# A convolution over normalized images: the next image's first points carried in the group matmul, bias by pairs, and one row of the last store in fourteen pieces

## The chip, the cores and the metric

The kernel runs on one core of a Trainium2 chip. The metric is the device time of one execution in microseconds; the median of 14 runs stands for the kernel. A separate, profiled execution gives the views that are read below; its span is counted from the first instruction to the last.

## The reference

The input x has 8 images of 32 channels and 128 x 128 points, in float32. Each image is group-normalized (16 groups of two channels, mean and variance over the group), convolved with a 3 x 3 kernel, a bias is added, and x itself is added:

```python
def _gn(v, G=16, eps=1e-5):
    g = v.reshape(B_, G, C_ // G, H_, W_)
    m = jnp.mean(g, axis=(2, 3, 4), keepdims=True)
    s = jnp.var(g, axis=(2, 3, 4), keepdims=True)
    return ((g - m) / jnp.sqrt(s + eps)).reshape(v.shape)

x = x + _L0_conv_ref(_gn(x), L0_conv_weight, L0_conv_bias, 1, 1)
```

The convolution of the reference is done by Fourier transform with a padding to 256 and a crop that is shifted against an ordinary "same" convolution. Of the cropped result only a corner holds products of the image; elsewhere the convolution is zero and the output is x plus the bias.

## The kernel before

**Layout.** The host arranges x so that a partition is one channel and one of the four parities of row and column: 32 x 4 = 128 partitions, each with H x W = 64 x 64 points of an image. Two images lie side by side as a pair, so there are NPAIR = 4 pairs and B = 8 images. Only the upper left N x N = 33 x 33 points of each image receive a convolution; the lower 31 rows ("low") and the right 31 columns of the upper 33 rows ("right") receive the bias alone.

**Loads and stores.** SyncE (SP) issues all of both, in one queue. Image 0 and image 1 come in halves of 1 MB, images 2 and 3 whole (2 MB), pairs 2 and 3 whole (4 MB each). All of x stays in the core's memory and is updated in place. Pairs 0 and 1 are stored whole, images 4, 5 and 6 one by one, image 7 in two parts: its low rows (`to[:, N:H, :]`), then the upper 33 rows (`to[:, 0:N, :]`), which is the last transfer.

**Statistics.** For each image VectorE sums the points (L275) and ScalarE the squares of the points less an origin (L294). The origin is the group's mean of the first point of each partition, the "pilot": GpSimd (POOL) copies the first points to a small tile (`take_first`, L247), TensorE multiplies them by the averaging matrix `avg` (`pilot`, L253), and ScalarE brings the product back (`pilot_back`, L283). Then `group` (L307) multiplies the two sums by `avg`, and a short chain between ScalarE and VectorE (L318 to L335) makes scale and shift. `normalize` (L349) writes the normalized corner g. GpSimd builds `avg` at the start (L205 to L225) and then the matrix of the weights (L440 to L448).

**Products.** `multiply` (L383) makes three chunks of 11 rows, each by four matrix products, into the four products' common place in PSUM; `add` (L399) adds the result and the bias to x on VectorE. `add_bias` (L367) adds the bias to low and right on GpSimd.

**Order.** `Queues` writes each engine's program in the order of the calls and turns dependencies into semaphore waits. In the loop over images TensorE does chunk 0 and three quarters of chunk 1 of image i, then the pilot of image i+2 and the group of image i+1, then the rest of image i. TensorE's instructions of the loop are kept and emitted as a hardware loop over the pairs (`emit_loop`): one common list of waits, whose values rise by a fixed step per pair. Before the loop TensorE runs three filler products of 512 columns (`keep_warm`, L417), set between the pilot of image 0, the two parts of image 0's group and the pilot of image 1:

```python
take_first(0); pilot(0); pilot_back(0); sum_up(0); sum_squares(0)
keep_warm(H // 2, 1, origin_ok[0])
group(0, 0)
keep_warm(H // 2, 1)
...
group(0, 1)
warm_ok = keep_warm(0, 1, w_ok)
pilot(1)
```

(The first five calls are on lines of their own in the kernel.)

Of the kernel before, what the change touches and what calls it, by code (L numbers as in the profile page):

```python
# [30 lines left out]
AF = mybir.ActivationFunctionType  # L31
ALU = mybir.AluOpType

P = 128
EPS = 1e-5
FFT = 256
FILL = 8
# [110 lines left out]
def conv_preact_kernel(nc: bass.Bass, x: bass.AP, wb: bass.AP, out: bass.AP):  # L148
    NPAIR, _, _, H, W = x.shape
    B = 2 * NPAIR  # L150
    C = P // 4
    LO = (FFT - 2 * H) // 4 - 1
    N = H - LO
# [3 lines left out]
    def sbuf(name, *shape):  # L157
        return nc.alloc_sbuf_tensor(name, list(shape), F32).ap()
# [36 lines left out]
    NUMBERS = 8 * H * W  # L195
    pair = sbuf("pair", P, P // 2, 2)
    w_sb = sbuf("w_sb", P, 4 * P)
    eps = sbuf("eps", P, 1)
    avg = sbuf("avg", P, P)
    warm = sbuf("warm", P, 1)  # L200
    idle = sbuf("idle", P, 1)
    bias_sb = sbuf("bias_sb", P, 1)
    pilots = [sbuf(f"pilot{k}", P, 1) for k in range(2)]
# [12 lines left out]
    sums = put(  # L216
        "pool", lambda e: e.tensor_add(avg[:, 0 : 2 * C], pair2[:, 0 : 2 * C], pair2[:, 2 * C : 4 * C]),
        pair_ok, mark=True,
    )
    sums = put(  # L220
        "pool", lambda e: e.tensor_add(avg[:, 2 * C : 3 * C], avg[:, 0:C], avg[:, C : 2 * C]), sums, mark=True
    )
    for k in (0, 1, 3):
        avg_ok = put(
            "pool", lambda e: e.tensor_copy(avg[:, k * C : (k + 1) * C], avg[:, 2 * C : 3 * C]), sums, mark=True  # L225
        )

    put("act", lambda e: e.activation(warm, eps, AF.Sqrt), eps_ok)  # L228

    gs = [sbuf(f"g{k}", P, N, N) for k in range(2)]  # L230
    sums = [sbuf(f"sums{k}", P, 2, 2) for k in range(2)]
    unused = sbuf("unused", P, H * W)
    origins = [sbuf(f"origin{img}", P, 1) for img in range(B + 1)]
    squares = [sbuf(f"square{img}", P, 1) for img in range(B)]
# [3 lines left out]
    pss = [psum(f"ps{k}", P, NCHUNK, BANK) for k in range(2)]  # L238
    ps_ms = psum("ps_m", P, BANK)
    ps_w = psum("ps_w", P, BANK)  # L240
    first_ok, pilot_ok, origin_ok, sums_ok, group_ok, means_read = {}, {}, {}, {}, {}, {}
    normal, conv_ok, biased, added = {}, {}, {}, {}

    def take_first(img, *needs):

        first_ok[img] = put(
            "pool", lambda e: e.tensor_copy(pilots[img % 2], xts[img][:, 0, 0:1] if img < B else eps),  # L247
            *(rows_in(img, 1) if img < B else ()), *needs, *([pilot_ok[img - 2]] if img > 1 else []), mark=True,
        )

    def pilot(img):
        pilot_ok[img] = put(
            "pe", lambda e: e.matmul(ps_w[:, 0:1], avg, pilots[img % 2], start=True, stop=True),  # L253
            first_ok[img], avg_ok, *([origin_ok[img - 1]] if img else []), mark=True,
        )

    def parts(img):

        return [slice(0, H // 2), slice(H // 2, H)] if img == 0 else [slice(0, H)]
# [8 lines left out]
    def sum_up(img):  # L268
        sums_ok.setdefault(img, [])
        for k, rows in enumerate(parts(img)):  # L270
            piece = xts[img][:, rows, :].rearrange("p h w -> p (h w)")
            sums_ok[img].append(
                put(
                    "dve",
                    lambda e: e.tensor_reduce(sums[img % 2][:, k, 0:1], piece, mybir.AxisListType.X, ALU.add),  # L275
                    *rows_in(img, rows.stop), *([group_ok[img - 2]] if img > 1 else []), mark=True,
                )
            )

    def pilot_back(img):  # L280
        origin_ok[img] = put(
            "act",
            lambda e: e.activation(origins[img], ps_w[:, 0:1], AF.Identity, scale=-float(NUMBERS // 8)),  # L283
            pilot_ok[img], mark=True,
        )

    def sum_squares(img):
        sums_ok.setdefault(img, [])
        for k, rows in enumerate(parts(img)):
            piece = xts[img][:, rows, :].rearrange("p h w -> p (h w)")  # L290
            sums_ok[img].append(
                put(
                    "act",
                    lambda e: e.activation(  # L294
                        unused[:, rows.start * W : rows.stop * W], piece, AF.Square, bias=origins[img],
                        accum_out=sums[img % 2][:, k, 1:2],
                    ),
                    origin_ok[img], *rows_in(img, rows.stop), *([group_ok[img - 2]] if img > 1 else []), mark=True,
                )
            )  # L300

    def group(img, part=0):

        last = len(parts(img)) - 1
        ok = put(
            "pe",
            lambda e: e.matmul(  # L307
                ps_ms[:, 0:2], avg, sums[img % 2][:, part, :], start=(part == 0), stop=(part == last)
            ),
            *(sums_ok[img][part :: last + 1]), avg_ok, *means_read.get(img - 1, ()), mark=part == last,  # L310
        )
        if part == last:
            group_ok[img] = ok
# [43 lines left out]
        pilot_back(img + 1)  # L357
        normal[img].append(origin_ok[img + 1])

    def add_bias(img):  # L360

        xt = xts[img]
        low = xt[:, N:H, :].rearrange("p h w -> p (h w)")
        right = xt[:, 0:N, N:W]
        free = [*normal[img], *sums_ok[img], bias_ok] + ([warm_ok] if img == 0 else [])
        biased[img] = [
            put("pool", lambda e: e.tensor_scalar(part, part, 1.0, bias_sb, op0=ALU.mult, op1=ALU.add), *free, mark=True)  # L367
            for part in (low, right)
        ]

    def multiply(img, n, products=range(4)):
        g = gs[img % 2]
# [33 lines left out]
    def store(to, of, *needs):  # L406
        return put("sp", lambda sp: sp.dma_start(to, of), *needs, adds="stored")
# [5 lines left out]
    def keep_warm(first, times, *needs):  # L413
        piece = xts[0][:, first : first + FILL, :].rearrange("p h w -> p (h w)")
        for _ in range(times):
            ok = put(
                "pe", lambda e: e.matmul(ps_w, avg, piece, start=True, stop=True),  # L417
                *rows_in(0, H), *needs, mark=True,
            )
        return ok  # L420

    take_first(0)
    pilot(0)
    pilot_back(0)
    sum_up(0)
    sum_squares(0)
    keep_warm(H // 2, 1, origin_ok[0])
    group(0, 0)
    keep_warm(H // 2, 1)

# [10 lines left out]
    for q in range(4):  # L441
        rin, cin = q // 2, q % 2
        to = slice(q * C, (q + 1) * C)
        bias_ok = put("pool", lambda e: e.tensor_copy(bias_sb[to, :], wb_sb[:, 15 * C : 15 * C + 1]), weights_in, mark=True)
        for dc, c, b in places[cin]:
# [5 lines left out]
                ),  # L451
                w_zero, weights_in, mark=True,
            )
    take_first(1, w_ok)
    group(0, 1)
    warm_ok = keep_warm(0, 1, w_ok)
    pilot(1)
    take_std(0)
    normalize(0)
    take_first(2)  # L460
    add_bias(0)
    sum_squares(1)
    sum_up(1)

# [3 lines left out]
    for img in range(B):  # L468
        multiply(img, 0)
        multiply(img, 1, range(3))  # L470
        if img:
            add(img - 1, 0, NCHUNK)
            if img == 2 or img == 4:
                store(out[img // 2 - 1], pairs[img // 2 - 1], *finished(img - 2, img - 1))
            elif img > 4:
                store(out[(img - 1) // 2, :, (img - 1) % 2], xts[img - 1], *finished(img - 1))
        pilot(img + 2)
        group(img + 1)
        multiply(img, 1, range(3, 4))
        if img + 1 < B:  # L480
            take_std(img + 1)
            normalize(img + 1)
            take_first(img + 3)
            add_bias(img + 1)
        multiply(img, 2)
        if img + 2 < B:
            sum_squares(img + 2)
            sum_up(img + 2)
        elif img + 2 == B:
            sum_nothing(B)  # L490
    xt, to = xts[B - 1], out[NPAIR - 1, :, 1]
    store(to[:, N:H, :], xt[:, N:H, :], biased[B - 1][0])
    add(B - 1, 0, 2)
    add(B - 1, 2, NCHUNK)
    stored = store(to[:, 0:N, :], xt[:, 0:N, :], biased[B - 1][1], *added[B - 1])


    put.emit_loop(NPAIR, {"act": 2 * 5, "dve": 2 * 5, "pool": 2 * 3})


    seen = {**put.seen["sp"]}
# [43 lines left out]
```

## Time and profile before

| what | value |
|---|---|
| median of 14 runs | 83.79 us (83.56 to 84.25) |
| the profiled execution's own time | 83.72 us |
| its span | 82.4 us |
| busy: TensorE, VectorE, ScalarE, GpSimd | 67.8, 50.1, 48.1, 32.2 us |
| DMA: moved, mean rate | 33.63 MB, 408 GB/s |
| chain that ended last: TensorE, DMA, ScalarE, VectorE | 74%, 8%, 7%, 3% |

Busy time is the time in which an engine had an instruction of its own under way. "PEld" is TensorE's weight load, which overlaps its products. The page divides the span into 40 slices and gives for each the busy share in tenths, and for DMA the mean share of 16 DMA engines. The chain of waits starts at the last compute instruction and follows it back to what released it; it ends where compute ends, and stores behind that are not in it. Windows give the same sums for any stretch of time. "SPq" is SyncE's queue, which only issues transfers.

### The profile page before, as it was taken

To read this page: it belongs to the slowest core of one execution; us is meant where nothing else is said; L and a number is where in the kernel's file an instruction comes from. 1 tells how busy PE (TensorE), PEld (TensorE's weight loads), DVE (VectorE), ACT (ScalarE), POOL (GpSimd) and SP (SyncE) were. 2 spreads that over 40 slices of the span, in tenths; PEclk is the share of its full clock that TensorE was granted. 3 is DMA by queue.
4 is the path that set the end of the run, shared out by engine and by line. 5 is a ranking of instruction groups with operands and counts; after the bars stand their busy time and mean duration, and the time that the engine had idled before them with its cause. 6 is when DMAs were issued, how large, how long until landed. Compare 5 with 4: busy or idle time off the path is not lost.

```text
span 82.4 us, 727 instructions
## 1 busy us (share of the span) xinstructions
PE 67.8 (82%) x238; PEld 43.1 (52%) x238; DVE 50.1 (61%) x43; ACT 48.1 (58%) x55; POOL 32.2 (39%) x52
## 2 busy tenths in 40 slices
PE   0002899898999999999999999999999999999000
PEld 0002455566666666676676666666766766665000
DVE  0019823990799399939967993999399636000700
ACT  6106942997699379739946993797399462000000
POOL 6709700009568000963920680095039106700000
PEclk9999999999999999999999999999999999999975
DMA  2899999999969969989969989989979999999994
GB/s 48 306 401 418 421 425 437 453 429 406 581 286 509 509 286 477 509 350 414 509 270 493 461 366 445 509 366 398 509 334 445 421 422 437 425 437 405 420 402 180
DMA packets 2209, 33.63 MB, mean 408 GB/s; under 512 B 256, under 2 KB 288, under 8 KB 416
## 3 DMA queue, kind: packets, MB, share of 16 engines
q1 hardware_dynamic: 2208, 33.62, 96.8%
q14 instruction: 1, 0.01, 0.0%
HBM read 16.84 MB, written 16.78 MB: 408 GB/s over the span
## 4 chain that ended last, share of the span: by engine, by line
PE 74%; DMA 8%; ACT 7%; DVE 3%; SPq 1%; issue 1%; ACTq 0%
PE ps L383 65%; DMA x<-x_dram 8%; PE ps_w L417 5%; ACT unused L294 5%; PE ps_m L307 3%; ACT g L349 2%; DVE x L399 2%; PE ps_w L253 1%; SPq L175 1%; ACT std L329 0%; ACT square L318 0%; DVE var L323 0%; DVE rstd L335 0%; DVE rstd L332 0%; ACT origin L283 0%
## 5 line engine op out<-in xcount | busy, mean ns | idle before, releaser
L383 PE MATMUL ps<-g,w_sb 128*128 128x363 f32 (+1 forms) x192 | 59.1, 463 | 0.2 <-ACT g L349 0.2
L383 PEld LDWEIGHTS ps<-g,w_sb 128*128 128x128 f32 x192 | 35.2, 189 | 19.4 <-ACT origin L283 1.6
L275 DVE TENSOR_REDUCE sums<-x 128x1 f32<-128x4096 f32 (+1 forms) x9 | 35.4, 3937 | 6.2 <-DMA x<-x_dram 6.2
L367 POOL TENSOR_SCALAR x<-x,bias_sb 128x1984 f32<-128x1984 f32 (+1 forms) x16 | 24.3, 1527 | 18.1 <-ACT origin L283 13.7
L294 ACT ACTIVATE unused<-x,origin 128x4096 f32<-128x4096 f32 (+1 forms) x9 | 30.0, 3330 | 0.3
L399 DVE SCALAR_TENSOR_TENSOR x<-ps,bias_sb,x 128x1089 f32<-128x1089 f32 (+2 forms) x9 | 10.9, 1219 | 7.9 <-PE ps L383 7.9
L349 ACT ACTIVATE g<-x,rstd 128x1089 f32<-128x1089 f32 (+2 forms) x9 | 10.7, 1203 | 3.9 <-DVE rstd L335 3.9
L247 POOL COPY pilot<-x 128x1 f32<-128x1 f32 x8 | 1.5, 184 | 20.3 <-DMA x<-x_dram 20.3
L253 PEld LDWEIGHTS ps_w<-pilot,avg 128*128 128x128 f32 x20 | 4.1, 209 | 9.0 <-POOL pilot L247 6.2
L253 PE MATMUL ps_w<-pilot,avg 128*128 128x1 f32 x20 | 3.1, 224 | 6.2 <-POOL pilot L247 6.2
L323 DVE TENSOR_SCALAR var<-ps_m,square 128x1 f32<-128x1 f32 x8 | 1.8, 219 | 10.5 <-ACT square L318 10.5
L417 PE MATMUL ps_w<-x,avg 128*128 128x512 f32 x6 | 6.0, 1108 | 1.8 <-DMA x<-x_dram 1.8
L318 ACT ACTIVATE square<-ps_m,origin 128x1 f32<-128x1 f32 x8 | 2.1, 261 | 8.7 <-PE ps_m L307 8.7
L307 PEld LDWEIGHTS ps_m<-sums,avg 128*128 128x128 f32 x20 | 3.8, 221 | 2.4 <-issue 1.9
L283 ACT ACTIVATE origin<-ps_w 128x1 f32<-128x1 f32 x9 | 1.4, 152 | 4.6 <-PE ps_w L253 4.6
L307 PE MATMUL ps_m<-sums,avg 128*128 128x2 f32 x20 | 3.8, 258 | 0.3 <-ACT unused L294 0.3
L329 ACT ACTIVATE std<-var,eps 128x1 f32<-128x1 f32 x8 | 2.4, 294 | 2.3 <-DVE var L323 2.3
L332 DVE RECIPROCAL rstd<-std 128x1 f32<-128x1 f32 x8 | 1.3, 164 | 2.9 <-ACT std L329 2.9
L417 PEld LDWEIGHTS ps_w<-x,avg 128*128 128x128 f32 x6 | 1.6, 325 | 1.9 <-issue 1.9
L448 POOL COPY w_sb<-wb_sb 32x128 f32<-32x128 f32 (+1 forms) x8 | 2.5, 339 | 0.0
L335 DVE TENSOR_SCALAR rstd<-ps_m,rstd 128x1 f32<-128x1 f32 x8 | 1.7, 218 | 0.3
L228 ACT ACT_TABLE_LOAD x1 | 1.3, 1283 | 0.8 <-PEq L534 0.8
(17 smaller groups left out, 7.0 us busy)
## 6 DMA issues: line engine op xcount, KB each, us to landing
x<-x_dram SPq DMA_DIRECT2D x2, 4096.0 KB, 33.5
out_dram<-x SPq DMA_DIRECT2D x2, 4096.0 KB, 15.1
out_dram<-x SPq DMA_DIRECT2D x3, 2048.0 KB, 7.3
x<-x_dram SPq DMA_DIRECT2D x4, 1024.0 KB, 7.8
x<-x_dram SPq DMA_DIRECT2D x2, 2048.0 KB, 17.4
out_dram<-x SPq DMA_DIRECT2D x1, 1056.0 KB, 4.5
out_dram<-x SPq DMA_DIRECT2D x1, 992.0 KB, 9.2
wb_sb<-wb_dram SPq DMA_DIRECT2D x1, 62.0 KB, 5.0
```

Of the source, the lines that this page charges most:

```text
L253: "pe", lambda e: e.matmul(ps_w[:, 0:1], avg, pilots[img % 2], start=True, stop=True),
L275: lambda e: e.tensor_reduce(sums[img % 2][:, k, 0:1], piece, mybir.AxisListType.X, ALU.add),
L294: lambda e: e.activation(unused[:, rows.start * W : rows.stop * W], piece, AF.Square, bias=origins[img], accum_out=sums[img % 2][:, k, 1:2],),
L307: lambda e: e.matmul(ps_ms[:, 0:2], avg, sums[img % 2][:, part, :], start=(part == 0), stop=(part == last)),
L318: lambda e: e.activation(squares[img], ps_ms[:, 0:1], AF.Square, bias=origins[img]),
L329: lambda e: e.activation(stds[img], variances[img], AF.Sqrt, bias=eps, scale=float(FFT * FFT)),
L349: lambda e: e.activation(g[:, rows, :], xt[:, LO + rows.start : LO + rows.stop, LO:W], AF.Identity, bias=rstd[:, 1:2], scale=rstd[:, 0:1],),
L367: put("pool", lambda e: e.tensor_scalar(part, part, 1.0, bias_sb, op0=ALU.mult, op1=ALU.add), *free, mark=True)
L383: lambda e, k=k, dc=dc, rows=rows, top=top: e.matmul(ps[:, 0:rows, 0 : N - dc], w_sb[:, k * P : (k + 1) * P], g[:, top : top + rows, dc:N] ...
L399: lambda e: e.scalar_tensor_tensor(part, in0=ps, scalar=bias_sb, in1=part, op0=ALU.add, op1=ALU.add),
L417: "pe", lambda e: e.matmul(ps_w, avg, piece, start=True, stop=True),
L448: lambda e: e.tensor_copy(w5[to, :, dc, :, c.start * C : c.stop * C], taps[:, 1 - rin : 5 - rin, b, :].rearrange("p (dr r) b o -> p dr r ( ...
```

## The change

- The tile of first points goes. The first point of image i+1 is written beside the sums of image i, as a third column, and the group product of image i brings back the next origin with its own two columns. Images 0 and 1 keep a pilot product, which reads x directly. Image 0's sums move to a tile of their own, as they come in two parts.
- `group` no longer stands behind a pilot in the loop; it waits for the copy of the next image's first points instead. `pilot_back` reads column 2 of the group's result from image 2 on. The copies that only kept the step even (from `eps`) go.
- The fillers read the first half of image 0 alone, write to another bank of PSUM (`pss[1]`), and two of them stand ahead of both group parts.
- `avg` is made by one addition of broadcast halves instead of one addition and three copies.
- `add_bias` takes images 0 and 1, and 2 and 3, as pairs; images 4 to 7 singly. The loop's step for GpSimd is 2 x 2 marks a pair instead of 2 x 3.
- Row N of image 7, which was the first of its low rows, is stored by 14 stores of 12, 14, 8, 10, 4, 15, 13, 9, 11, 6, 2, 7, 16 and 1 partitions (128 in all, 256 bytes each), between the low rows and the last store.

```diff
-    sums = put("pool", ... tensor_add(avg[:, 0 : 2 * C], pair2[:, 0 : 2 * C], pair2[:, 2 * C : 4 * C]) ...)
-    sums = put("pool", ... tensor_add(avg[:, 2 * C : 3 * C], avg[:, 0:C], avg[:, C : 2 * C]) ...)
-    for k in (0, 1, 3):
-        avg_ok = put("pool", ... tensor_copy(avg[:, k * C : (k + 1) * C], avg[:, 2 * C : 3 * C]) ...)
+    pair_ok = put("pool", ... tensor_add(half, pair2[:, 0 : 2 * C], pair2[:, 2 * C : 4 * C]) ...)
+    avg_ok = put("pool", lambda e: e.tensor_add(
+            avg.rearrange("p (q c) -> p q c", q=4), *(
+                half[:, k * C : (k + 1) * C].unsqueeze(1).to_broadcast([P, 4, C]) for k in range(2)
+            )), pair_ok, mark=True)
...
-    sums = [sbuf(f"sums{k}", P, 2, 2) for k in range(2)]
+    first_sums = sbuf("first_sums", P, 2, 2)
+    sums = [sbuf(f"sums{k}", P, 3) for k in range(2)]
...
     def take_first(img, *needs):
         first_ok[img] = put(
-            "pool", lambda e: e.tensor_copy(pilots[img % 2], xts[img][:, 0, 0:1] if img < B else eps),
-            *(rows_in(img, 1) if img < B else ()), *needs, *([pilot_ok[img - 2]] if img > 1 else []), mark=True,
+            "pool", lambda e: e.tensor_copy(sums[(img - 1) % 2][:, 2:3], xts[img][:, 0, 0:1]),
+            *rows_in(img, 1), *needs, *([group_ok[img - 3]] if img > 3 else []), mark=True,
         )
     def pilot(img):
         pilot_ok[img] = put(
-            "pe", lambda e: e.matmul(ps_w[:, 0:1], avg, pilots[img % 2], start=True, stop=True),
-            first_ok[img], avg_ok, *([origin_ok[img - 1]] if img else []), mark=True,
+            "pe", lambda e: e.matmul(ps_w[:, img : img + 1], avg, xts[img][:, 0, 0:1], start=True, stop=True),
+            *rows_in(img, 1), avg_ok, mark=True,
         )
+    def to_sum(img, part):
+        return first_sums[:, part, :] if img == 0 else sums[img % 2]
...
     def pilot_back(img):
+        of = ps_w[:, img : img + 1] if img < 2 else ps_ms[:, 2:3]
...
-            pilot_ok[img], mark=True,
+            pilot_ok[img] if img < 2 else group_ok[img - 1], mark=True,
...
     def group(img, part=0):
-                ps_ms[:, 0:2], avg, sums[img % 2][:, part, :], start=(part == 0), stop=(part == last)
+                ps_ms[:, 0 : of.shape[1]], avg, of, start=(part == 0), stop=(part == last)
             ),
-            *(sums_ok[img][part :: last + 1]), avg_ok, *means_read.get(img - 1, ()), mark=part == last,
+            *(sums_ok[img][part :: last + 1]), *([first_ok[img + 1]] if img and img + 1 < B else []),
+            avg_ok, *means_read.get(img - 1, ()), mark=part == last,
...
-    def add_bias(img):
+    def add_bias(*imgs):
+        xt = pairs[imgs[0] // 2] if len(imgs) == 2 else xts[imgs[0]].unsqueeze(1)
+        low = xt[:, :, N:H, :].rearrange("p b h w -> p b (h w)")
+        right = xt[:, :, 0:N, N:W]
...
-                "pe", lambda e: e.matmul(ps_w, avg, piece, start=True, stop=True),
-                *rows_in(0, H), *needs, mark=True,
+                "pe", lambda e: e.matmul(pss[1][:, 0, :], avg, piece, start=True, stop=True),
+                *rows_in(0, first + FILL), *needs, mark=True,
...
-    take_first(0)
     pilot(0)
     pilot_back(0)
     sum_up(0)
     sum_squares(0)
-    keep_warm(H // 2, 1, origin_ok[0])
+    keep_warm(0, 2)
     group(0, 0)
-    keep_warm(H // 2, 1)
...
-    take_first(1, w_ok)
...
-    take_first(2)
-    add_bias(0)
+    take_first(2, w_ok)
...
-        pilot(img + 2)
         group(img + 1)
...
-            take_first(img + 3)
-            add_bias(img + 1)
+            if img < B - 4:
+                take_first(img + 3)
+            if img == B - 5:
+                take_first(img + 4)
+            if img in (0, 2):
+                add_bias(img, img + 1)
+            elif img > 2:
+                add_bias(img + 1)
...
-    store(to[:, N:H, :], xt[:, N:H, :], biased[B - 1][0])
+    store(to[:, N + 1 : H, :], xt[:, N + 1 : H, :], biased[B - 1][0])
+    base = 0
+    for number in (12, 14, 8, 10, 4, 15, 13, 9, 11, 6, 2, 7, 16, 1):
+        part = slice(base, base + number)
+        store(to[part, N : N + 1, :], xt[part, N : N + 1, :], biased[B - 1][0])
+        base += number
...
-    put.emit_loop(NPAIR, {"act": 2 * 5, "dve": 2 * 5, "pool": 2 * 3})
+    put.emit_loop(NPAIR, {"act": 2 * 5, "dve": 2 * 5, "pool": 2 * 2})
```

More of the change, by code (lines that the diff above doesn't have):

```diff
@@ L198, in conv_preact_kernel @@
     eps = sbuf("eps", P, 1)
+    half = sbuf("half", P, 2 * C)
     avg = sbuf("avg", P, P)
@@ L202, in conv_preact_kernel @@
     bias_sb = sbuf("bias_sb", P, 1)
-    pilots = [sbuf(f"pilot{k}", P, 1) for k in range(2)]
     eps_ok = put("pool", lambda e: e.memset(eps, EPS * FFT * FFT), mark=True)
@@ L215, in conv_preact_kernel @@
     pair2 = pair.rearrange("p a b -> p (a b)")
-    sums = put(
-        "pool", lambda e: e.tensor_add(avg[:, 0 : 2 * C], pair2[:, 0 : 2 * C], pair2[:, 2 * C : 4 * C]),
+    pair_ok = put(
+        "pool", lambda e: e.tensor_add(half, pair2[:, 0 : 2 * C], pair2[:, 2 * C : 4 * C]), pair_ok, mark=True
+    )
+    avg_ok = put(
+        "pool",
+        lambda e: e.tensor_add(
+            avg.rearrange("p (q c) -> p q c", q=4), *(
+                half[:, k * C : (k + 1) * C].unsqueeze(1).to_broadcast([P, 4, C]) for k in range(2)
+            )
+        ),
         pair_ok, mark=True,
     )
-    sums = put(
-        "pool", lambda e: e.tensor_add(avg[:, 2 * C : 3 * C], avg[:, 0:C], avg[:, C : 2 * C]), sums, mark=True
-    )
-    for k in (0, 1, 3):
-        avg_ok = put(
-            "pool", lambda e: e.tensor_copy(avg[:, k * C : (k + 1) * C], avg[:, 2 * C : 3 * C]), sums, mark=True
-        )
     put("act", lambda e: e.activation(warm, eps, AF.Sqrt), eps_ok)
     gs = [sbuf(f"g{k}", P, N, N) for k in range(2)]
-    sums = [sbuf(f"sums{k}", P, 2, 2) for k in range(2)]
+    first_sums = sbuf("first_sums", P, 2, 2)
+    sums = [sbuf(f"sums{k}", P, 3) for k in range(2)]
     unused = sbuf("unused", P, H * W)
@@ L274, in sum_up @@
                     "dve",
-                    lambda e: e.tensor_reduce(sums[img % 2][:, k, 0:1], piece, mybir.AxisListType.X, ALU.add),
+                    lambda e: e.tensor_reduce(to_sum(img, k)[:, 0:1], piece, mybir.AxisListType.X, ALU.add),
                     *rows_in(img, rows.stop), *([group_ok[img - 2]] if img > 1 else []), mark=True,
@@ L280, in pilot_back @@
     def pilot_back(img):
+        of = ps_w[:, img : img + 1] if img < 2 else ps_ms[:, 2:3]
         origin_ok[img] = put(
             "act",
-            lambda e: e.activation(origins[img], ps_w[:, 0:1], AF.Identity, scale=-float(NUMBERS // 8)),
-            pilot_ok[img], mark=True,
+            lambda e: e.activation(origins[img], of, AF.Identity, scale=-float(NUMBERS // 8)),
+            pilot_ok[img] if img < 2 else group_ok[img - 1], mark=True,
         )
@@ L295, in sum_squares @@
                         unused[:, rows.start * W : rows.stop * W], piece, AF.Square, bias=origins[img],
-                        accum_out=sums[img % 2][:, k, 1:2],
+                        accum_out=to_sum(img, k)[:, 1:2],
                     ),
@@ L304, in group @@
         last = len(parts(img)) - 1
+        of = to_sum(img, part)
         ok = put(
@@ L358, in normalize @@
         normal[img].append(origin_ok[img + 1])
-    def add_bias(img):
[L362 to L368, printed above, removed]
-        ]
+    def add_bias(*imgs):
+        xt = pairs[imgs[0] // 2] if len(imgs) == 2 else xts[imgs[0]].unsqueeze(1)
+        low = xt[:, :, N:H, :].rearrange("p b h w -> p b (h w)")
+        right = xt[:, :, 0:N, N:W]
+        free = [token for img in imgs for token in (*normal[img], *sums_ok[img])]
+        free += [bias_ok] + ([warm_ok] if 0 in imgs else [])
+        marks = (len(imgs) == 2 or imgs[0] >= B - 2, True)
+        tokens = [
+            put("pool", lambda e: e.tensor_scalar(part, part, 1.0, bias_sb, op0=ALU.mult, op1=ALU.add), *free, mark=mark)
+            for part, mark in zip((low, right), marks)
+        ]
+        for img in imgs:
+            biased[img] = [token for token in tokens if token]
     def multiply(img, n, products=range(4)):
@@ L491, in conv_preact_kernel @@
     xt, to = xts[B - 1], out[NPAIR - 1, :, 1]
-    store(to[:, N:H, :], xt[:, N:H, :], biased[B - 1][0])
+    store(to[:, N + 1 : H, :], xt[:, N + 1 : H, :], biased[B - 1][0])
[4 more added lines that the diff above has]
+        base += number
+    assert base == P
     add(B - 1, 0, 2)
```

## The prediction, as it was written before the changed kernel ran

> **What bounds the kernel now.** I read the chain of waits first, since it names the work that ended last, then the DMA rows of the page, the end in half-microsecond windows, and the store queue. Chain (start us, us, what):
>
> ```profile
> 65.43 0.12 PE ps_w L253 x2
> 65.55 0.22 PE ps_m L307 x2
> 65.77 7.22 PE ps L383 x24
> 72.99 0.12 PE ps_w L253 x2
> 73.10 0.23 PE ps_m L307 x2
> 73.33 3.02 PE ps L383 x10
> 76.34 0.03 issue
> 76.37 1.48 DVE x L399 x2
> ```
>
> It says that TensorE is back to back from 20.05 us on: 7.22 us of products, 0.12 of pilot, 0.22 of group per image. But it follows compute instructions only; its last one ends at 77.85 of a span of 82.4. What lies behind is DMA, and the page shows DMA full long before (tenths and GB/s in 40 slices of 2.06 us, then the queue's share):
>
> ```profile
> DMA  2899999999969969989969989989979999999994
> GB/s 48 306 401 418 421 425 437 453 429 406 581 286 509 509 286 477 509 350 414 509 270 493 461 366 445 509 366 398 509 334 445 421 422 437 425 437 405 420 402 180
> ...
> q1 hardware_dynamic: 2208, 33.62, 96.8%
> ```
>
> 33.62 MB at the 425 GB/s of the middle are 79 us, and the first packet starts at 1.8 us. So two resources are full at once, and the end tells which one counts. The windows there (us, length, busy time of PE, PEld, DVE, ACT, POOL; clock, DMA share, GB/s):
>
> ```profile
> 77.50:78.00 0.50, 0.00 (x0) 0.00 (x0) 0.34 (x1) 0.00 (x0) 0.00 (x0) 1.00 1.09 460
> 78.00:78.50 0.50, 0.00 (x0) 0.00 (x0) 0.00 (x0) 0.00 (x0) 0.00 (x0) 1.00 0.94 397
> 78.50:79.00 0.50, 0.00 (x0) 0.00 (x0) 0.00 (x0) 0.00 (x0) 0.00 (x0) 1.00 0.76 316
> 79.00:79.50 0.50, 0.00 (x0) 0.00 (x0) 0.00 (x0) 0.00 (x0) 0.00 (x0) 0.90 1.16 489
> ...
> 81.00:81.50 0.50, 0.00 (x0) 0.00 (x0) 0.00 (x0) 0.00 (x0) 0.00 (x0) 0.50 0.50 203
> 81.50:82.00 0.50, 0.00 (x0) 0.00 (x0) 0.00 (x0) 0.00 (x0) 0.00 (x0) 0.50 0.04 17
> ```
>
> Here the reader is to see two things. The only hole is 0.76 at 78.5. The trace's single packets (not shown) explain it: the last store is issued at 77.87, its first packets start at 78.70, and the DMA engines that had finished the store before it, from 78.41 on, stood idle up to 0.3 us. The 0.04 at 81.5 is one engine alone: 0.04 x 16 x 0.5 = 0.32 us, one 8448-byte packet. That straggler ends at 81.86, the others between 81.30 and 81.54. It lands last (82.34 against 81.94), and it finished the previous store at 79.32, when the last one was already in its ring: **it had no hole at all.** It fell behind on its own packets, about 625 ns for 16,384 bytes where the others take 611. The store queue confirms that nothing upstream starves it:
>
> ```profile
> SPq L407 <- DVE x L399: 41.9, 6, 8.5
> SPq L87 <- POOL x L367: 28.2, 3, 21.3
> SPq L508 <- DMA out_dram<-x: 4.2, 1, 4.2
> ```
>
> SP waits long for DVE, yet each earlier store is issued 1 us or more before the rings run dry: image 6's at 70.19, while image 5's drains until 71.5. So the bound is the straggler's own bytes, with TensorE some 0.6 us behind: only if the last issue came later than about 78.5 would the straggler itself wait.
>
> **What the Trainium skill says.** "DMA: Bandwidth & Descriptors", section on why a DMA increments its semaphore by 16: a store from SP runs on the lowest-numbered k of the 16 engines, k the largest number up to 16 dividing the rows. No store of 12 or 14 rows is in the trace of before; the 128-row packets fit k = 16. The same page's "Latency and other measured facts" calls engines 7 and 15 usually slower; the trace shows one slow engine, but not its number. Its "Specifications" put the smallest line-rate transfer at 512 bytes, with a read-modify-write below; no such data packet is in this trace. "TensorE: Matmul & The Clock Gate", Part 1: 3.4 us of activity, in a free-running window, release the full clock. It agrees: fillers from 8.63 us run about 2.0 us each, and full clock is granted from 14.55.
>
> **The change, part by part.**
>
> *Prologue.* Pilot 0 reads x directly: PE starts it at the landing, 5.97, not at 6.24 behind POOL's copy (0.19 us). Squares of image 0 then end near 10.9, not 11.15. The fillers move ahead of both groups and need the first half only: from 6.6, two at 2.04 end at 10.7; group parts at 0.22 end near 11.2, where before 13.04. ACT's chain moves 1.8 us: squares of image 1 end at 18.2 instead of 19.93. But group 1 now also waits for take_first(2), which waits for image 2: POOL starts that copy at 18.49 now, so 18.67 plus 0.05 gives group 1 at 18.75 instead of 20.05. Gain on TensorE 1.3 us; **late next is the load of image 2.** The matrix: one 128-wide addition, from the 64- and 32-wide rows (0.317, 0.252) about 0.45 us, replaces 0.25 + 0.50; avg is ready near 3.5 instead of 3.9, hidden by the first load until 5.97.
>
> *Loop.* The pilot pair leaves: 0.12 us x 7 between group 1 and group 8 = 0.84. A third column in the group costs next to nothing: one column is 224 ns (L253), two are 258 (L307), and both overlap their neighbours. TensorE ends 2.1 us earlier, 74.2, and the last add at 75.7. ACT's squares (26.98) precede the group (27.62) by 0.64, so 0.12 is covered; g follows the group at the same distance as before.
>
> *POOL.* Bias by pairs has the same elements: 2 x (1.92 + 1.13) = 6.1 us. Pair 0-1 starts behind take_first(3), 23.3 (image 3's landing), and ends at 29.5; its store waits for DVE until 33.4 anyway. Queued behind it is take_first(4), which needs pair 2, landed 33.0: first point at 33.2, group 3 due at 33.6, so 0.4 us to spare. Pair 2-3: 36.9 to 43.0, its store due at 48.5. The loop's common wait plan makes group 7 wait for the lower bias part of image 6, done some 5.1 us after group 6; the groups are 7.43 apart. All hidden; without cover each would delay TensorE, which has 2.1 + 0.6 us to lose before the end moves.
>
> *Tail.* Row 33 of the last image (256 bytes per partition) leaves the 7936-byte store and goes as 14 stores. On SP: issues cost 0.33 to 0.51 us; 14 x 0.42 = 5.9, after image 7's bias, 68.55 + 0.43: 69.0 to 74.9 (76.1 at 0.51). The last store is due at 75.7 and needed at about 77.5: hidden; it would decide from 0.6 us each. On the engines: from k lowest-numbered, engine 0 gets 14 packets, 7 gets 9, 15 gets 1, where each had 8 rows inside long packets (8 x 256 B at 0.037 ns/B = 75 ns). A short packet is unseen. Lower bound, from the line through 1984 bytes (78 ns) and 16,384 (607): 14.5 ns; upper, the 1984-byte packet, 78; I take 20. A semaphore packet each adds 6. So engine 0: 14 x 26 - 75 = +0.29 us (bounds +0.21 to +1.1); engine 7: 9 x 26 - 75 = +0.16 (+0.11 to +0.68); engine 15: 26 - 75 = -0.05 (-0.055 to +0.01). The earlier last issue closes the hole for the early engines, worth up to 0.3 us to them and **0 to the straggler**.
>
> **Sum.** 2.1 us saved on TensorE, worth 0; straggler -0.05 if it is engine 15: span 82.35, and 83.67 with the 1.32 us around it. The profiled 83.72 stands 0.07 under the median of 83.79, so 83.74 on that scale; I write 83.7.
>
> **Rivals.**
> 1. *Short packets decide* (slower). If the straggler is engine 7, or the packets cost 40 ns, where engine 0 with 14 x 46 - 75 = +0.57 passes it from an ordinary end: +0.16 to +0.68, say 84.15. For it: read-modify-write, more packets; against: engine 0 passes the straggler only from about 36 ns up (81.35 + 14 x 42 ns - 0.075 = 81.86), and engine 15 is as likely the slow one as 7. Chance 0.27.
> 2. *TensorE is late in many unprofiled runs* (faster). The 14 times fall near 83.6, 83.8 and 84.1; a clock window released later would delay TensorE beyond its 0.6 us. Then its earlier end takes the 84.1 group down: 83.45. Against: the profiled run is no such run. Chance 0.20.
> 3. *The chain is right as it stands*: 83.72 - 2.1 = 81.6. Against: 96.8% of DMA. Chance 0.03.
>
> The main forecast keeps 0.50. A difference of 0.3%, 0.25 us, is about what a measurement of this kernel can tell from none: faster by more 0.23, within 0.50, slower 0.27. Likeliest case alone: 83.5 to 84.0. The range with rivals 1 and 2 is 83.3 to 84.2.
>
> **What would show it.** Right: last compute ends near 75.7, the dip at 78.5 is gone, DMA stays full until 81.5, last landing about 82.3; group 1 near 18.75, released by POOL; 14 issues of about 0.4 us ending before 76.2. Wrong: a landing before 81.9 (the straggler depended on something else), an issue of the last store after 77.5, 256-byte packets above 36 ns, a group waiting in the loop.

## The result, and the profile after

| what | before | after |
|---|---|---|
| median | 83.80 us (83.56 to 84.50, 47 runs) | 85.25 us (85.02 to 85.66, 10 runs) |
| the profiled execution's own time | 83.72 us | 85.05 us |
| its span | 82.4 us | 83.7 us |
| last compute instruction ends | 77.85 us | 75.13 us |
| last store issued | 77.87 us | 79.59 us |
| first packet of the last store | 78.70 us | 80.44 us |
| last landing | 82.34 us | 83.65 us |

The ratio is 1.017, with a 95% interval of 1.0148 to 1.0193: the change makes the kernel slower by 1.45 us. (Some executions of one and the same kernel fall in a state that is some 2% slower; ratios and intervals, here and below, compare the others alone, so they need not be the quotient of the medians.) The forecast, 83.7 us with a range up to 84.2, was wrong. Compute ends 2.7 us earlier, and the last store leaves 1.7 us later.

The chain of waits of the kernel after (start us, us, what):

```profile
63.13 0.14 PE ps_m L317 x2
63.27 7.22 PE ps L399 x24
70.49 0.12 PE ps_m L317 x2
70.61 3.01 PE ps L399 x10
73.62 0.03 issue
73.65 1.48 DVE x L415 x2
```

The pilot rows are gone, and the last addition ends at 73.65 + 1.48 = 75.13. So the compute side did what it was meant to do. The chain ends 8.6 us ahead of the end of the span, so the loss can't be in it. The DMA rows and the queue's line of the page:

```profile
DMA  2899999999996998999799899889969999999566
GB/s 47 321 383 427 419 419 458 438 407 454 517 454 297 501 501 360 391 501 470 282 501 423 376 454 501 376 376 501 501 282 446 423 431 438 431 423 405 212 260 258
DMA packets 2464, 33.62 MB, mean 402 GB/s; under 512 B 512, under 2 KB 544, under 8 KB 672
q1 hardware_dynamic: 2464, 33.62, 95.4%
```

The bytes are the same. 37 slices look like those of before; the last three hold 5 to 6 tenths. In half-microsecond windows (us, length, busy time of PE, PEld, DVE, ACT, POOL; clock, DMA share, GB/s):

```profile
78.00:78.50 0.50, 0.00 (x0) 0.00 (x0) 0.00 (x0) 0.00 (x0) 0.00 (x0) 0.50 0.88 339
78.50:79.00 0.50, 0.00 (x0) 0.00 (x0) 0.00 (x0) 0.00 (x0) 0.00 (x0) 0.50 0.30 64
79.00:79.50 0.50, 0.00 (x0) 0.00 (x0) 0.00 (x0) 0.00 (x0) 0.00 (x0) 0.50 0.05 8
79.50:80.00 0.50, 0.00 (x0) 0.00 (x0) 0.00 (x0) 0.00 (x0) 0.00 (x0) 0.50 0.05 9
80.00:80.50 0.50, 0.00 (x0) 0.00 (x0) 0.00 (x0) 0.00 (x0) 0.00 (x0) 0.50 0.32 135
80.50:81.00 0.50, 0.00 (x0) 0.00 (x0) 0.00 (x0) 0.00 (x0) 0.00 (x0) 0.50 0.97 406
```

From about 78.8 to 80.4 us little more than short packets of row 33 runs; the last packet of the low rows ends at 79.15. Every compute engine is idle, its work long done, and 1 MB waits to be stored. In the kernel before, the last store was already running from 78.70 on. Why it isn't here is read from the issues of SyncE's stores (L423): minimum, median and maximum in ns, then the starts. The three lines come from the windows 68.1 to 77.1, 77.15 to 79.5 and 79.5 to 85; an issue that overlaps a window's edge is counted in it, so the 1026 of the second line is the last one of the first.

```profile
L423 SPq DMA_DIRECT2D out_dram<-x x8: 1026/1102/1125, 68.1 to 76.1; - x8
L423 SPq DMA_DIRECT2D out_dram<-x x8: 253/305/1026, 76.1 to 79.2; - x8
L423 SPq DMA_DIRECT2D out_dram<-x x1: 360/360/360, 79.6 to 79.6; - x1
```

The low rows and the first seven pieces take 1.03 to 1.13 us each, the other seven 0.25 to 0.32. The pieces occupy SyncE from 69.24 to 79.49, and the last store, whose data are ready at 75.13, stands behind them. In the kernel before, the same view of the last three stores (image 6, the low rows, the upper rows) shows:

```profile
L407 SPq DMA_DIRECT2D out_dram<-x x3: 332/332/426, 70.2 to 77.9; - x3
```

### The profile page after: what moved, and what is told of

It reads as the page before. It is cut to its first block, busy times and chain, and to the rows that moved or that the text cites. A ratio compares the mean times of both kernels' runs of the same rounds, so it can differ in the third digit from the quotient of the medians.

```text
span 83.7 us, 698 instructions
## 1 busy us (share of the span) xinstructions
PE 67.0 (80%) x222; PEld 41.6 (50%) x222; DVE 50.2 (60%) x43; ACT 48.0 (57%) x55; POOL 30.3 (36%) x41
## 4 chain that ended last, share of the span: by engine, by line
PE 75%; DMA 6%; ACT 5%; DVE 2%; issue 0%
PE ps L399 70%; DMA x<-x_dram 6%; ACT unused L302 5%; PE ps L433 2%; PE ps_m L317 2%; DVE x L415 2%; PE ps_w L257 1%; ACT origin L291 0%
## 5 line engine op out<-in xcount | busy, mean ns | idle before, releaser
L282 DVE TENSOR_REDUCE sums<-x 128x1 f32<-128x4096 f32 x7 | 30.9, 4410 | 0.6 <-DMA x<-x_dram 0.6
L381 POOL TENSOR_SCALAR x<-x,bias_sb 128x1984 f32<-128x1984 f32 (+3 forms) x12 | 23.3, 1951 | 17.3 <-ACT origin L291 13.0
L282 DVE TENSOR_REDUCE first_sums<-x 128x1 f32<-128x2048 f32 x2 | 4.6, 2285 | 6.3 <-DMA x<-x_dram 6.3
L250 POOL COPY sums<-x 128x1 f32<-128x1 f32 x6 | 1.0, 185 | 18.3 <-DMA x<-x_dram 18.3
L433 PE MATMUL ps<-x,avg 128*128 128x512 f32 x6 | 5.8, 1108 | 0.0
L317 PEld LDWEIGHTS ps_m<-sums,avg 128*128 128x128 f32 x16 | 2.7, 188 | 2.3 <-DVE x L415 1.0
L291 ACT ACTIVATE origin<-ps_w 128x1 f32<-128x1 f32 x2 | 0.3, 160 | 4.4 <-PE ps_w L257 4.4
L317 PE MATMUL ps_m<-sums,avg 128*128 128x3 f32 x16 | 2.4, 219 | 0.0
L433 PEld LDWEIGHTS ps<-x,avg 128*128 128x128 f32 x6 | 1.8, 334 | 1.0 <-issue 1.0
L317 PEld LDWEIGHTS ps_m<-first_sums,avg 128*128 128x128 f32 x4 | 1.2, 325 | 1.6 <-ACT unused L302 1.1
```

The source lines that it names most:

```text
L282: lambda e: e.tensor_reduce(to_sum(img, k)[:, 0:1], piece, mybir.AxisListType.X, ALU.add),
L317: lambda e: e.matmul(ps_ms[:, 0 : of.shape[1]], avg, of, start=(part == 0), stop=(part == last)),
L433: "pe", lambda e: e.matmul(pss[1][:, 0, :], avg, piece, start=True, stop=True),
```

## The experiments

Each is compared with the kernel before on the same chip. Chips differ, so the kernel before has its own median in each case: 84.27 us for e1 to e4, 83.94 for e5 to e8, 84.17 for e9 to e12. Runs without an interval have a profile and few times; their times are given, but the argument uses the profile.

### The change in two halves

e1 is the kernel before with nothing but the pieces; e2 is the changed kernel without them.

```diff
 e1, against before:
-    store(to[:, N:H, :], xt[:, N:H, :], biased[B - 1][0])
+    store(to[:, N + 1 : H, :], xt[:, N + 1 : H, :], biased[B - 1][0])
+    for number in (12, 14, 8, 10, 4, 15, 13, 9, 11, 6, 2, 7, 16, 1): ...one store each
 e2, against after: the same lines the other way round
```

> The kernel before with only the tail of the change: row N of image 7 in 14 stores. Theory A (the queue of SyncE runs ahead of the DMA engines by only some 22 descriptors per engine, data and completion counted; an issue beyond that lasts as long as two packets of 16 KB, 1.1 us): the first piece goes in about 0.35 us, the next four or five take 1.1 us each until image 6's store has drained at 76.4, the others 0.35; the last store is issued near 79.9 instead of 77.9, and the run takes 85.3 to 85.7. Theory B (two instructions in a row cost 1.1 us each as long as 16 KB packets are under way, whatever their size): last issue near 80 as well. Theory C (the loss comes from the new order on TensorE and GpSimd): 83.8, as before.

Measured: 86.24 us, ratio 1.0227 (1.0183 to 1.0272). The issues behind image 6's store, low rows first, last store last:

```profile
L407 SPq DMA_DIRECT2D out_dram<-x x16: 253/364/1216, 71.1 to 81.2; - x16
```

Here the low rows take 422 ns, the first six pieces 0.92 to 1.22 us, the rest 0.25 to 0.37; the last store leaves at 81.23, though its own last addition has ended at 78.31, and the windows show the hole (us as above):

```profile
80.00:81.00 1.00, 0.00 (x0) 0.00 (x0) 0.00 (x0) 0.00 (x0) 0.00 (x0) 0.50 0.09 23
81.00:82.00 1.00, 0.00 (x0) 0.00 (x0) 0.00 (x0) 0.00 (x0) 0.00 (x0) 0.50 0.03 5
82.00:83.00 1.00, 0.00 (x0) 0.00 (x0) 0.00 (x0) 0.00 (x0) 0.00 (x0) 0.50 0.96 406
```

> The changed kernel with row N of image 7 put back into its low rows, one store: all of the change but its tail. Theory A and B: SyncE is free, the last store is issued at the end of the last addition, near 75.2, and does not wait; no hole in the DMA engines, the one slow engine sets the end near 81.85, 83.6 to 83.8. Theory C: 85.2, as the changed kernel.

Measured: 84.23 us, ratio 0.9977 (0.9943 to 1.0012). The low rows still take 1052 ns, but only one store stands behind them; it leaves at 75.27, and the place of the hole is full:

```profile
78.50:79.00 0.50, 0.00 (x0) 0.00 (x0) 0.00 (x0) 0.00 (x0) 0.00 (x0) 0.50 1.11 464
79.00:79.50 0.50, 0.00 (x0) 0.00 (x0) 0.00 (x0) 0.00 (x0) 0.00 (x0) 0.50 1.04 439
79.50:80.00 0.50, 0.00 (x0) 0.00 (x0) 0.00 (x0) 0.00 (x0) 0.00 (x0) 0.50 0.96 406
```

Run again as e12, against another chip's runs:

> The kernel of e2 once more, for its time: the change without its tail. If the DMA engines bound the end in nearly every run, 2.4 us less on TensorE bring nothing: ratio 0.997 to 1.002. If many runs of the kernel before are held up by TensorE: 0.993 or lower.

Measured: 84.01 us, ratio 0.9993 (0.9962 to 1.0023). What follows from the three: the pieces carry the whole loss, and everything else in the change, with 2.7 us less on TensorE's side, brings nothing that can be measured. Rival 2 of the prediction, that TensorE is late in many runs (83.45 us, a ratio of 0.996), isn't supported, though e2's interval doesn't exclude it. The ratio is larger in e1 than with the whole change; its pieces begin 2.3 us later (71.55 against 69.24).

### Issue, packets or completions: the pieces elsewhere

Three runs keep row 33 apart from the low rows, but not as 14 issues ahead of the last one on SyncE.

```diff
 e3:  store(...) of each piece -> put("act", lambda e: e.dma_start(to, of), ...)
 e4:  the loop -> store(to[:, N : N + 1, :], xt[:, N : N + 1, :], biased[B - 1][0])
 e6:  the loop behind the last store, which no longer waits for it
```

> The changed kernel with the 14 pieces issued by ScalarE, which has nothing left to do by then, so that they go through its own queue. Theory A: that queue is empty, each issue takes 0.3 to 0.4 us, and SyncE issues the last store near 75.2: 83.7. Theory B: ScalarE takes 1.1 us for each, but the last store is still issued near 75.2: 83.7 too; the length of the issues tells A from B.

Measured: 84.43 us, ratio 1.0027 (0.9993 to 1.0061): the loss is gone with the same 14 stores of the same bytes. On ScalarE their issues occupy 11.3 us (timeline of ScalarE):

```profile
70.24 11.32 ACTq L426 DMA_DIRECT2D out_dram<-x  x14
```

Nine of the 14 take over 0.5 us, up to 1.21, in a queue that held nothing else. But the last store on SyncE isn't behind them and leaves at 77.26, when its data are ready. So it is the order on one issuing engine that costs the time, and a store's long issue is no property of SyncE's own queue. The Trainium skill ("DMA: Bandwidth & Descriptors", "Issuing engines are not separate DMA queues") says that issuing from several engines only saves the time to initiate a DMA, "which is usually small relative to the DMA itself". The first half agrees; the second doesn't here, with up to 1.2 us of issue for packets of 18 ns.

> The changed kernel with row N of image 7 as one store of all 128 partitions: 8 packets of 256 bytes and a completion on each engine, 9 descriptors, in one issue instead of 14. Theory A: this issue waits for 9 descriptors to leave, 4 to 5 us, and the last store's issue is long as well, ending near 77.9; 83.7 to 84.0. Theory B: 1.1 us, and the last store at 75.2 is short, 0.35 us; 83.7. Theory D (stores on fewer than 16 engines are what is slow): 0.35 us for both.

Measured: four times, 83.51, 83.64, 85.10 and 85.42 us, too scattered for a ratio (the kernel before has 83.60 to 85.59 on that chip); the profiled run, of 83.64 us, has a span of 82.3 us, without a hole. Its issue of row 33 alone:

```profile
L423 SPq DMA_DIRECT2D out_dram<-x x1: 1026/1026/1026, 69.7 to 69.7; - x1
```

One store of 128 rows of 256 bytes takes 1.03 us, where the store of four took 1.11. So some 1.1 us is the price of an issue here, not of its packets, and not of room for them in the queue: that theory asked for 4 to 5 us from a store with eight packets for each engine.

> The changed kernel with its 14 pieces issued behind the last store instead of ahead of it; nothing else moved. If the loss is that the last store's issue stood behind them: it leaves near 75.3, the hole in the DMA engines is gone, the pieces (one or two at 1.1 us, the rest 0.35) are all issued before 81.5, and the end is 83.7 to 84.0, level with the kernel before on the same chip. If small packets cost the DMA engines time, the loss of 1.4 us stays.

Measured: 85.77 us, ratio 1.0204 (1.0149 to 1.0258). The last large store leaves at 75.71 and its packets end at 81.8. The pieces behind it (their 14 issues):

```profile
L423 SPq DMA_DIRECT2D out_dram<-x x14: 253/315/1177, 76.1 to 82.6; - x14
```

Three take 0.70 to 1.18 us, the rest 0.25 to 0.37, and they land at 84.6. The expectation missed: the loss stays, by another road, as now their own chain of issues ends last. As to the hole, e6 confirms it: without issues ahead of it the large store isn't late.

### Fewer pieces: a second cost

```diff
-    for number in (12, 14, 8, 10, 4, 15, 13, 9, 11, 6, 2, 7, 16, 1):
+    for number in 8 * (16,):
```

> The changed kernel with row N of image 7 in 8 stores of 16 partitions each instead of 14 uneven ones. If the loss is the number of issues behind the full queue (1.1 us each while 16 KB packets are under way, 0.35 after): low rows and seven pieces at 1.1 us end near 77, the eighth 0.35, the last store near 77.6 just in time: a level with the kernel before (83.7 to 84.0, or 84.2 to 84.5 on a chip that runs like the last one). If it is the uneven numbers of partitions, stores on fewer than 16 engines: each takes 0.35 us, the last store leaves near 75.3, and the time is the same; only the lengths of the issues tell the two apart.

Measured: 85.07 us, ratio 1.0115 (1.0078 to 1.0152). The low rows and the eight pieces:

```profile
L423 SPq DMA_DIRECT2D out_dram<-x x9: 701/955/1021, 68.3 to 76.3; - x9
```

Pieces over all 16 engines are as slow to issue, so the odd counts are not the reason. With eight the last store leaves at 77.07 and starts at 78.58, in time, as the prediction's limit of 77.5 has it. And still there is a loss. The windows of its end show where:

```profile
79.50:80.00 0.50, 0.00 (x0) 0.00 (x0) 0.00 (x0) 0.00 (x0) 0.00 (x0) 0.50 1.35 389
80.00:81.00 1.00, 0.00 (x0) 0.00 (x0) 0.00 (x0) 0.00 (x0) 0.00 (x0) 0.50 1.08 194
81.00:82.00 1.00, 0.00 (x0) 0.00 (x0) 0.00 (x0) 0.00 (x0) 0.00 (x0) 0.50 0.87 355
```

From 80 to 81 the engines are counted busy (1.08) and move 194 GB/s: packets stand in the engines without moving. Single packets of the last store take up to 968 ns there (median 319). Over the same stretch, 78.8 to 81.0, the semaphore counts of the pieces' completions arrive one by one, 13.3 ns apart, whichever engine they come from: 128 of them are 1.7 us. In the kernel after most of them fall into the hole, where no data of the last store stand beside them. The single records also show a control: e4 sends the same 128 packets of 256 bytes over the same time (from 78.3 and 78.4 us), but with 16 completions instead of 128. Its last store's packets all took 319 ns, and its window from 80 to 81 moves 414 GB/s:

```profile
80.00:81.00 1.00, 0.00 (x0) 0.00 (x0) 0.00 (x0) 0.00 (x0) 0.00 (x0) 0.50 0.98 414
```

So the short packets aren't what holds the data up in e5. It comes with the number of stores and of their completions, which no run here separates; that it is the completions is argued from the times, not shown.

### What makes an issue slow

The theories on record come down to four: the issue waits for packets in flight to end (one of 16 KB every 607 ns); it waits for a number of entries in the queue; any DMA is slow to issue beside busy engines; or only stores behind stores are. The probes leave the pieces out, and add other transfers or sizes.

```diff
 e7 (no pieces):  + 16 loads of 16 x 256 bytes into a spare tile, while the loads of images 1 to 5 run
 e9 (no pieces):  + the same 16 loads with one partition each, + 4 loads behind the low rows
 e10 (no pieces): + 6 stores of one partition at 30 us, ahead of pair 0's store
 e8:  8 pieces of 16 partitions, ahead of the low rows, after image 5's store has landed
 e11: images 5 and 6 stored in halves of 8 KB a partition, then the 14 pieces
```

> The changed kernel without pieces, and with 16 added loads of 16 partitions x 256 bytes into an unused tile, whose issue lengths are the measurement: 6 when image 1 has landed (13.5 us, 16 KB packets under way, some 35 descriptors per engine queued), 6 when image 3 has (23.3 us, 32 KB packets, 18 queued), 4 when pair 2 has (33.0 us, 32 KB packets, 9 queued). If an issue waits for about two packets of the size under way: 1.1 us, 2.2 us and 2.2 us, from the second of each burst on. If it waits on a count of queued descriptors (over some 15 to 22): the first burst slow, the second slow or mixed, the third all short, 0.35 us. If only stores are held up: 0.35 to 0.45 us everywhere. The time itself should stay within 0.3 us of the kernel before.

> The changed kernel with row N of image 7 in 8 stores of 16 partitions, issued ahead of the low rows and only after image 5's store has landed (near 72.3 us), so that 9 descriptors per engine are queued instead of 16, with 16 KB packets under way. If a count of queued descriptors decides (15 or more): the first three or four issues take 0.35 us, the later ones 1.1. If the size of the packets under way decides: 1.1 us from the second on. The low rows then leave late and the DMA engines run dry for a while, so the time is 1 to 5 us longer and is not the question.

> As e7 (added loads of 256 bytes per partition in three bursts of 6, 6 and 4), but each of one partition, so that it runs on one DMA engine and brings one completion instead of 16; and 4 more such loads directly behind the low rows, near 69 us, with stores under way. If the 2.6 us that e7 lost are the completions, 256 of them one after the other at 13.5 ns (3.4 us): 16 cost 0.2 us, and the time is level with the kernel before. If a short transfer costs the engines a fixed time however many rows it has: the loss of e7 stays. The four late issues: 1.1 us each if whatever is issued behind the queued stores is slow; 0.42 us if only the issue of stores is.

> The changed kernel without its pieces, and with 6 added stores of one partition (256 bytes, of image 0's row N) issued near 30 us, with loads of 32 KB packets under way and 16 to 20 descriptors per engine queued; pair 0's store waits for them, so it comes some 1 us late behind the loads and the time is about 1 us longer. If the issue of a store is slow only behind queued stores: 0.3 to 0.42 us each. If the issue of any store into a filled queue is slow: 1.1 us or more from the second on.

> The changed kernel with its 14 pieces, and the stores of images 5 and 6 in two halves of 8 KB packets each instead of one of 16 KB. If an issue lasts until two packets of the size under way have left: 0.6 us each, the last store leaves near 78 instead of 79.6, and the loss shrinks from 1.4 us to 0.3 to 0.8 us. If 1.1 us is a time of its own: the issues keep 1.1 us, and the loss stays at 1.4 us or grows by the two added stores.

Measured, the issues:

| run | issues | ns |
|---|---|---|
| e7 | 16 loads of 16 partitions, behind 16 KB and 32 KB load packets | 311 to 422 |
| e9 | 16 loads of one partition, behind loads | 223 to 289 |
| e9 | 4 loads, behind stores | 248 to 301 |
| e10 | 6 stores, behind loads | 247 to 309 |
| e8 | 8 stores with few stores queued: second, then the rest | 784, then 419 to 422 |
| e11 | second halves, low rows and six pieces, behind stores; then a seventh piece | 1012 to 1144; 543 |

The last two in the view of SyncE's stores (first e8, its eight pieces and the low rows; then e11 from 68 to 76.85, with one of its two second halves):

```profile
L425 SPq DMA_DIRECT2D out_dram<-x x9: 330/420/784, 73.1 to 77.0; - x9
L423 SPq DMA_DIRECT2D out_dram<-x x9: 543/1037/1144, 68.0 to 76.8; - x9
```

None of the added loads is slow, nor the stores behind loads. Stores are slow directly behind a deep queue of stores, with the exceptions below. One issue of the kernel's own loads can be slow as well: the ninth in a row at the start took 513 ns in the kernel after, but 834 in e1, 1022 in e3 and 1044 in e10. So a long issue is not stores' alone; bursts have it in common. In e11 the packets ahead are half as long (8 KB, some 0.3 us) and the issue is not shorter, so it doesn't wait for one or two packets to end. In e8 stores with full-size packets still under way are issued in 0.42 us. The depth of the queue comes nearest. The low rows' own issue stands directly behind image 6's store in all kernels but e8 and e11. Counted from single packets (not shown), at its start 9.7 to 12.3 data packets were issued and not yet ended per engine, on the mean, in the kernel before, e1, e3, e4 and e9, and it took 419 to 461 ns; in the kernel after, e2, e5, e6, e10 and e12 they were 13.1 to 14.1, and it took 750 to 1211. So the time saved on TensorE works against the issues: image 6's store leaves at 67.69 in the kernel after, where it left at 70.19, with more still queued ahead of it. But no fixed number fits: e7's low rows took 420 ns with 17.8, a piece in e8 784 ns with 6.7, and two in e3 some 340 ns with about 18. **What exactly the issue waits for stays open**; no law was found that fits all the runs.

As times: e11 was 85.45 us, ratio 1.0204 (1.0143 to 1.0264), the loss of the pieces once more. e8 (84.85 us once) ran dry at 76 to 78 us, since its pieces and low rows wait for image 5's store, and e10 (85.47 us once) held pair 0's store up; neither says anything of the loss. e7 took 86.59 us, once. Its 256 added completions at 13.3 ns are 3.4 us, and the window in which they arrive shows the engines full and slow:

```profile
40.00:45.00 5.00, 5.00 (x20) 3.21 (x19) 3.86 (x5) 3.40 (x7) 3.61 (x5) 1.00 1.05 230
```

At 420 GB/s, 230 GB/s over 5 us are 2.3 us lost. e9, with 20 completions in place of 256, moves 381 GB/s from 40 to 45 us, and the kernel after 419. That supports the second cost of e5. But e9 was not level: 85.37 us, ratio 1.0185 (1.0129 to 1.0242). At its end one or two engines alone are busy; all its probes were on one engine, but a cause isn't shown.

## Why the prediction was wrong, point by point

**The bound: right.** Stores bound the end. TensorE's saving was said to be worth nothing, and e2 and e12 measure nothing. In the kernel after, though, the end was set not by the straggler's own bytes, as forecast, but by when the last store was issued.

**Prologue and loop: right in time, with one size off and one wait not shown.** The group parts end at 11.59 (11.2). Group 1 starts at 18.86 (18.75 forecast). It was to be released by the copy of image 2's first point, which ends at 18.71, but the chain has TensorE's own products up to the group, without a gap:

```profile
13.73 5.29 PE ps L399 x14
19.02 0.19 PE ps_m L317 x2
```

The same 14 products took 4.48 us before. The full clock is granted at 15.40, where it was granted at 14.55, though the fillers start 2.1 us earlier. So products and copy were about level, and the good time is luck in part. The period from group to group is 7.34 us where it was 7.55, so a pilot less is worth 0.21 us an image, not 0.12: in the chain the group beside it takes 0.12 to 0.14 us as well, where it took 0.22. The last addition ends at 75.13 (75.7). The matrix's one addition takes 0.45 us as estimated. The bias by pairs takes 5.54 us (6.1), and no group in the loop waits for it. TensorE's third column is unseen.

**The packets: right; their completions: not.** A short packet is recorded at 18 ns. The prediction's 78 and 607 ns are times from start to start (the packets themselves are recorded at 81 and 611); by that measure its completion follows after 14 ns (bounds 14.5 to 78, 20 taken) and the next packet after 20, where 26 was used. So the packets lie on the line of the longer ones, and no read-modify-write shows in them. Rival 1, that short packets decide, fell with it; it gave 84.15 us, the right side for the wrong reason. Packets carry no engine number in these traces, so engines 0, 7 and 15 of that sum came to no test. A completion takes the 6 ns of its own engine that were priced for it. But their counts arrive 13.3 ns apart for all engines together, 1.7 us for the 128, which no term of the sum has. In the kernel after most of this falls into the hole. In e5, with the last store in time and as many completions, the ratio is still 1.0115, about 1.0 us. An estimate from this: with cheap issues the time would have been near 84.8 us, outside the range as well.

**SyncE: here it failed.** The step was: "14 x 0.42 = 5.9, after image 7's bias, 68.55 + 0.43: 69.0 to 74.9 (76.1 at 0.51). The last store is due at 75.7 and needed at about 77.5: hidden; it would decide from 0.6 us each." The pieces began at 69.24, so the start was right. From there to the last store's issue at 79.59 are 10.35 us, 0.74 each: seven at 1.03 to 1.13 (7.65 us together), seven at 0.25 to 0.32 (2.04), and 0.66 between them. The break-even of 0.6 was named, and 0.74 lies beyond it; the duration was mis-sized. 0.33 to 0.51 was the spread of issues in the trace of before: its longest are nine loads in a row into an empty queue, and of its stores one alone is issued directly behind another (426 ns, with 9.9 packets per engine to go). Fourteen in a row behind queued stores is a thing that trace doesn't hold. The packets were bounded from both sides for that reason, and the issues were not. The hidden wait became the deciding one.

**The size follows from it.** The last store's packets start at 80.44, not 78.70: 1.74 us. The last packet ends at 83.26, not 81.86: 1.40 us, against 1.3 of span and 1.45 between the medians. The difference fits the straggler, which finished the previous store late in the kernel before and could catch up in the hole; which engine ends last isn't recorded. The up to 0.3 us that the earlier issue was to give the early engines never came, as the issue was later.

**The rivals as a set.** The slower side got 0.27, all of it on packets on the engines. That the 14 issues hold back the last store, from 0.6 us each, was written down as a condition and given no chance.

## What to carry to other kernels

Count DMA issues as work of the issuing engine, in order: what stands behind them is late by their sum, and an issue's duration in a sparse trace is no price for a burst of stores behind queued stores. Where the break-even is within a factor of two of the price used, give it a chance of its own. Small stores belong into a larger one (one issue for 128 rows cost what one for four did) or onto an engine that has nothing urgent behind them, and expect a cost of many small stores besides, as e5 shows.

## What the runs showed of the hardware that I had not expected

- A store's issue took 0.25 to 0.46 us in most places, and mostly 0.8 to 1.2 us directly behind a deep queue of stores (the low rows from 13.1 data packets per engine on, though not in e7), whether it carried 1 KB or 1 MB, on 4 or 128 partitions, from SyncE or from ScalarE. The loads added behind loads and behind stores stayed at 0.22 to 0.42 us, but the ninth load of the first burst took up to 1.04. What sets it is open.
- Completion counts of pieces arrived 13.3 ns apart over all engines together. 128 of them are 1.7 us, and data packets beside them took up to three times their median (968 against 319 ns). The same 128 short packets with 16 completions (e4) slowed nothing.
- Packets of 256 bytes from the core's memory to DRAM were recorded at 18 ns, 14 from start to start, where the line through the longer ones gives 14.5: they show no penalty of their own.
